# Making the shifted neighbour numbers on GpSimd instead of VectorE in a four-layer graph network

## The chip, the cores and the metric

The kernel runs on one core of one Trainium2 chip. The core has five engines that matter here: TensorE (PE, matrix products into PSUM), VectorE (DVE), ScalarE (ACT), GpSimd (POOL) and SyncE (SP, which issues nearly all DMAs). The metric is the device time of one execution in microseconds. Kernels are compared by the median of several runs.

## The reference, cut to what matters

128 graphs of 128 nodes with 64 features go through four layers, each `x = x + layer(max(layernorm(x), 0))`. Layer 0 is an edge network over the neighbours of each node; layers 1 to 3 multiply by the dense adjacency matrices and small weights.

```python
# layer 0, per graph; h is the normed input, mask = adj > 0
h_e = relu(xj_proj[:, None, :] + (h[:, None, :] - h[None, :, :]) @ W1b + b1)   # 192 wide
hm  = sum over neighbours k of h_e[j, k] * mask[j, k]
out = hm @ W2 + deg * b2
# layer 1: three graph convolutions relu(adj @ (h @ W + b)), then an output product
# layer 2: (adj @ h + h) @ W + b, rows scaled to length 1, batch norm over all graphs
# layer 3: tanh(concat(h, adj @ h) @ W1 + b1) @ W2 + b2
```

About an eighth of the entries of the adjacency matrices are nonzero, and the diagonal always is. Layer 0 is computed over the neighbours that are there, not over all pairs.

## The kernel before

**Tiling.** The graphs are worked in 32 groups of G = 4. A tile has the 128 nodes on the partitions, and the four graphs side by side. Layer 0 to layer 2 of all groups run in one software pipeline; layer 3 follows, because layer 2 has a batch norm over everything.

**Layer 0.** For every node the kernel numbers its neighbours. It sorts the rows by how many neighbours they have left beyond the first few, so that late neighbour slots are needed by few rows. The stage `sort` makes the tiles for this: `to` and `fro` (permutations into and out of the sorted order), `num` (for sorted row and column, the neighbour's number) and `num_r`. `num_r` is the tile of this case. Its 128 columns are cut into six segments of SEGS = 76, 33, 11, 4, 2 and 2 columns; every segment holds the first columns of `num` with a multiple of 3 taken off. One comparison with a constant then selects neighbour n in the first segment's rows, n + 3 in the second's, and so on. Four instructions make the first four segments (304, 132, 44 and 16 elements a partition, for four graphs); a fifth, with an operand `behind`, makes the last two together (16 elements).

The stage `pick` makes one-hot tiles by comparing `num`, `num_r` or `near_n` with a constant, all on VectorE. From group 1 on the twelve of a group come in this order: near 0, other 0, other 1, near 1, other 2, other 3, near 2, other 4, other 5, near 3, other 6, other 7. The near ones write `ohn` from `near_n` (`num` rearranged by way of DRAM); the others write `oh`, from `num` for other 0 to 4 and from `num_r` for other 5, 6 and 7.

Each group then has 40 half tiles (20 neighbour slots by two pairs of graphs), which go through five PSUM banks `blk`:

- `fill`: ScalarE copies `psort` (or `psort_r`, for the segments) into a bank;
- `subtract`: TensorE adds one-hot times `near_q` or `q` into the bank;
- `gather`: VectorE takes the relu and adds it to `acc` (half tiles 26 and 27 go by ScalarE).

Half tile h + 5 can be filled when half tile h is gathered. Below, "`acc` 23" is the VectorE instruction that gathers half tile 23. The stage `project` makes `q` and `psort` from the normed input (`x`, `sq`, `var`, `rstd`, `h`, `hT`); on GpSimd it makes the third part of `q`, `db` and `x+db`. The stage `after_layer0` ends layer 0 and does layers 1 and 2 (`sA`, `sB`, `ah`, `dT`, `msg`, `t`, `h`, `zT`, `sqy`, `nrm`, `counted`, `y`); its GpSimd work is `x+t`, `adjT+ident`, the mean's `x` and `y*nrm`.

**The order on the engines.** `keep_in_program_order` makes each engine run its instructions in the order in which they are emitted. That order comes from a timetable written out by hand. Each stage of each group is a generator; each piece up to the next `yield` has a due time (units of about 10 ns) from a plan, added to the group's start. Groups start PERIOD apart. `run_all` always emits the piece that is due first among those whose gate is open: a free PSUM bank, a tile made, a half tile gathered.

```python
    def due(self):
        k = min(self.k, len(self.plan) - 1)
        return self.start + self.scale * (self.plan[k] + 40 * (self.k - k))
...
        while streams:
            s = min((s for s in streams if s.gate is None or s.gate()), key=lambda s: s.due())
            s.step()
```

`sort` and `project` of a group run one period ahead of its half tiles, `after_layer0` one to two periods behind. The last entry of SORT_PLAN is the due time of `num_r`. First and last groups have other starts, scales and plans (MOVED, OWN); the change leaves these as they are.

Of the kernel before, what the change touches and what calls it, by code (L numbers as in the profile page):

```python
# [14 lines left out]
ALU = mybir.AluOpType  # L15
# [16 lines left out]
BLOCKS = 3  # L32
SEGS = [76, 33, 11, 4, 2, 2]
STARTS = [sum(SEGS[:s]) for s in range(len(SEGS))]
# [11 lines left out]
MOVED = {('pick', -1): (0, 0.75), ('pick', -2): (-109, 1.102), ('fill', -1): (18, 0.75), ('fill', -2): (0, 1.021), ('subtract', -1): (-1, 0.752), ('subtract', -2): (21, 0.988), ('gather', -1): (0, 0.75), ('gather', -2): (20, 1.0), ('pick', 0): (-1203, 0.997), ('fill', 0): (-119, 0.877), ('subtract', 0): (-65, 0.947), ('gather', 0): (-52, 0.511), ('sort', 0): (-364, 0.972), ('sort', 1): (-635, 0.697), ('project', 0): (691, 0.585), ('project', 1): (155, 0.997), ('after_layer0', 0): (0, 1.0), ('first_half', -1): (-602, 0.992), ('second_half', -1): (-112, 1.0)}  # L46
OWN = {('after_layer0', -2): [-734, -65, 691, 691, 691, 691, 691, 972, 1066, 1154, 1255, 1280, 1280, 1440, 1566, 1644, 1757, 1757, 1940, 1940, 2090, 2450, 2450, 2450, 2450, 2685, 2837, 2881, 3086, 3128, 3145, 3290, 3290, 3290, 3438, 3438, 3592, 3592, 3627, 3646, 3684, 3976, 4078, 4109, 4421, 4485, 4512, 4899], ('first_half', -1): [-1189, -966, -886, -871, -753, -659, -570, -311, -230, -110, -107, -26, -26, 24, 49, 159, 231, 233, 351, 355, 454, 465, 465, 520, 582, 606, 717, 717, 879, 909, 909, 998, 1084, 1149, 1238, 1238, 1283, 1313, 1390, 1404, 1404, 1660, 1664, 1695, 1824, 1984, 2001, 3035], ('second_half', -1): [-1130, -987, -834, -703, -655, -586, -484, -231, -231, -231, -109, -52, -17, 45, 104, 176, 245, 361, 361, 365, 470, 482, 482, 541, 607, 632, 750, 783, 934, 968, 968, 1168, 1168, 1222, 1321, 1321, 1368, 1391, 1493, 1493, 1493, 1734, 1786, 1832, 1980, 2117, 2144, 2459], ('sort', 0): [-361, 30, 30, 595, 607, 607, 738, 738, 860, 860, 860, 1135, 1135, 1235, 1331, 1331, 2024, 2074, 2074, 2134, 2159, 2159], ('project', 0): [-1241, -907, -868, -728, -442, 1053, 1192, 3091, 3728, 3875, 4077, 4162, 4162, 4162, 4182, 4512, 4589, 4619, 4619, 4651, 4662, 4902, 4978, 4996, 5074, 5127, 5127, 5664, 5780], ('pick', -1): [-1123, -774, -706, -706, -634, -425, -425, -96, -84, 631, 881, 881, 896, 1076, 1084, 1544, 1671, 1732, 2021, 2039, 2044, 2391, 2680, 2783, 2937, 3043]}
SET_UP_PLAN = [93, 1417, 1908, 1908, 2104, 2104, 3420, 4777]
PERIOD = 3386
SORT_PLAN = [-154, -48, 199, 202, 627, 627, 627, 929, 958, 958, 1091, 1091, 1251, 1452, 1457, 1527, 1567, 1663, 1680, 1736, 2145, 2323]  # L50
PROJECT_PLAN = [-3200, -3200, -3091, -3000, -2654, -2409, -881, 903, 903, 1198, 1371, 1474, 1614, 1698, 1832, 2224, 2239, 2239, 2335, 2335, 2471, 2516, 2579, 2723, 2943, 2976, 3375, 3417, 3511]
PICK_PLAN = [-1127, -907, -707, -689, -679, -577, -388, -388, -388, -31, 176, 734, 734, 1933]
FILL_PLAN = [-1179, -835, -192, -192, -192, -16, 194, 226, 527, 527, 666, 706, 715, 853, 1221, 1303, 1303, 1303, 1303, 1303, 1676, 1686, 1802, 1837, 1891, 1913, 1913, 1921, 1977, 2170, 2328, 2636, 2799, 2799, 2824, 2828, 2857, 2994, 2994, 3161, 3181]
SUBTRACT_PLAN = [-578, -369, -369, -369, -257, -40, -28, 354, 738, 738, 937, 937, 952, 952, 1114, 1123, 1130, 1476, 1567, 1688, 1688, 1746, 1860, 1936, 1978, 2041, 2068, 2293, 2349, 2448, 2623, 2758, 2868, 2868, 2926, 2939, 2939, 3072, 3078, 3201, 3238]
GATHER_PLAN = [-821, -801, -426, -156, -156, 267, 444, 479, 589, 589, 589, 1159, 1159, 1370, 1476, 1616, 1654, 1654, 1699, 1699, 1981, 1981, 2115, 2265, 2434, 2445, 2445, 2478, 2478, 2516, 2516, 2533, 2675, 2675, 2809, 2809, 2809, 2809, 2812, 2812, 2812]
AFTER_PLAN = [-115, -109, 110, 147, 311, 768, 891, 1024, 1031, 1342, 1462, 1486, 1666, 1825, 1907, 2009, 2138, 2138, 2250, 2401, 2571, 2571, 2663, 2805, 2902, 2973, 3117, 3221, 3537, 3748, 3892, 3907, 4155, 4155, 4155, 4239, 4331, 4381, 4557, 4586, 4665, 4760, 4834, 4915, 5251, 5412, 5494, 5494]
WARM = 15
BEHIND = 2
SPLIT = 1
# [49 lines left out]
def network(ctx, tc, io, out, over=None, x1=None):  # L109

    nc = Engines(tc)
# [218 lines left out]
    def set_up_first():  # L330

        yield
        nc.vector.tensor_scalar(wq, wp, -1.0, None, ALU.mult)
        nc.vector.tensor_tensor(wp, wp, wtop, ALU.add)
        done.add("w")
        yield
        centred(b2_all, F)
        yield from split_part(where["L0_gnn_b1"])
        for t in (near_q[1:] + near_n[1:]):
            nc.gpsimd.memset(t, 0.0)  # L340
        done.add("first")
        yield
# [191 lines left out]
    def sort(g):  # L534
# [70 lines left out]
        num = edge.tile([P, G, P], BF16, tag="num", name="num")  # L605
# [19 lines left out]
        yield  # L625
        num_r = edge.tile([P, G, P], BF16, tag="num_r", name="num_r")
        for i in range(LIKE):
            nc.vector.tensor_scalar(num_r[:, :, STARTS[i] : STARTS[i] + SEGS[i]], num[:, :, 0 : SEGS[i]], float(-i * BLOCKS), None, ALU.add)
        m, n = len(SEGS) - LIKE, SEGS[LIKE]
        nc.vector.tensor_tensor(  # L630
            num_r[:, :, STARTS[LIKE] : P].rearrange("p b (m n) -> p b m n", n=n),
            num[:, :, 0:n].unsqueeze(2).to_broadcast([P, G, m, n]),
            behind.unsqueeze(1).unsqueeze(3).to_broadcast([P, G, m, n]),
# [400 lines left out]
    if x1 is not None:  # L1034
        run(set_up_first())
        run(set_up())
        for g in range(NG - 1):
            run(after_layer0(g))
    else:
        streams = []  # L1040
        early = -9 * PERIOD
        streams.append(Stream(set_up_first(), SET_UP_PLAN, early))
        streams.append(Stream(set_up(), REST_PLAN, 0))
        for g in range(NG):
            for stage, plan, start in (
                (sort, SORT_PLAN, (g - 1) * PERIOD if g else early),
                (project, PROJECT_PLAN, (g - 1) * PERIOD if g else early),
                (pick, PICK_PLAN, g * PERIOD),
                (fill, FILL_PLAN, g * PERIOD),
                (subtract, SUBTRACT_PLAN, g * PERIOD),  # L1050
                (gather, GATHER_PLAN, g * PERIOD),
                *(((after_layer0, AFTER_PLAN, (g + 1) * PERIOD),) if g < NG - SPLIT else ((first_half, AFTER_PLAN, (g + 1) * PERIOD), (second_half, AFTER_PLAN, (g + 1) * PERIOD))),
            ):
                key = stage.__name__, g if g < 2 else g - NG
                later, scale = MOVED.get(key, (0, 1.0))
                streams.append(Stream(stage(g), OWN.get(key, plan), start + later, scale))
        streams.append(Stream(squares(), SQUARES_PLAN, (NG - 1) * PERIOD))
        streams.append(Stream(filler(), FILLER_PLAN, (NG - 1) * PERIOD))
        run_all(streams)
# [316 lines left out]
```

## Time and profile before

| what | value |
|---|---|
| median of 3 runs | 1288.45 us (1286.49 to 1288.77) |
| the profiled execution: its time | 1288.35 us |
| its span, first to last instruction | 1286.6 us |
| mean granted TensorE clock | 0.972 |
| instructions | 31407 |
| DVE `num_r`, the five forms together | 40.4 us busy in 160 instructions |

The profile is of one execution. Its time is 1.75 us longer than its span. A row such as `L93 DVE TENSOR_SCALAR num_r<-num 128x304 bf16<-128x304 bf16 x32 | 7.4, 230 | 0.0` reads: line, engine, operation, tile written <- tiles read, shapes, how many | busy us in all, mean ns of one | us that the engine stood idle just before them. The line is L93 for nearly all, since one helper emits everything, so the tiles tell the rows apart. `[0.47 <-PE blk L93]` in a timeline means that the engine stood idle 0.47 us until TensorE's `blk` was done.

### The profile page before, as it was taken

Reading aid. Unit: us, or ns where it says so; the run is one execution under the profiler, and the core shown is the slowest. Engines: PE = TensorE matmul, PEld = TensorE weight load, DVE = VectorE, ACT = ScalarE, POOL = GpSimd, SP = SyncE. Lnnn points to the kernel's source line nnn. Section 1 sums busy time; section 2 is a strip of 40 time slices with the busy share of each in tenths; the row PEclk is TensorE's granted clock in tenths of the full one; section 3 lists DMA queues with packets and bytes.
Section 4 is the critical chain, followed back from the end, with each engine's and each line's share of the span. In section 5 each row is a group of like instructions: output and inputs, shape, how many; then the busy total and the mean of one; then the engine's idle time right before and its main releaser. Section 6 shows DMA issues by size and latency. Waiting matters only on the chain.

```text
span 1286.6 us, 31407 instructions
## 1 busy us (share of the span) xinstructions
PE 1159.5 (90%) x10989; PEld 982.1 (76%) x10990; DVE 1158.9 (90%) x3204; ACT 1034.2 (80%) x2583; POOL 318.4 (25%) x400
## 2 busy tenths in 40 slices
PE   5689999999999999999999999999999999888697
PEld 2568888888877887787878878888878887767576
DVE  6889999999999999999999999999999998845993
ACT  3678888888988888888888888888988888743576
POOL 4241122212121222222211222221211222021992
PEclk9899999999999999999999999999999999995899
DMA  2222222222222222222222222222222212100264
GB/s 80 81 76 70 73 67 73 76 76 77 76 76 69 71 74 66 66 74 71 72 74 71 68 71 72 77 76 76 77 76 67 70 59 61 30 17 1 79 160 128
DMA packets 107012, 92.53 MB, mean 72 GB/s; under 512 B 45135, under 2 KB 90460, under 8 KB 106844
## 3 DMA queue, kind: packets, MB, share of 16 engines
q1 hardware_dynamic: 106380, 90.17, 24.7%
q8 instruction: 89, 1.46, 0.5%
q14 instruction: 79, 0.65, 0.2%
q10 hardware_dynamic: 464, 0.26, 0.1%
HBM read 34.12 MB, written 16.71 MB: 40 GB/s over the span
## 4 chain that ended last, share of the span: by engine, by line
ACT 40%; PE 35%; DVE 16%; issue 4%; POOL 2%; SPq 2%; DMA 1%; DVEq 0%; ACTq 0%; POOLq 0%
ACT blk L93 22%; PE blk L93 14%; PE ps_pr L93 7%; DVE acc L93 4%; ACT extra L93 3%; PE ps_q L93 3%; PE ps_ag L93 3%; ACT dT L93 3%; ACT msg L93 2%; PE ps_ah L93 2%; DVE var L93 2%; ACT psort L93 2%; PE ps_ga L93 2%; PE ps_endps L93 2%; SPq L93 2%
## 5 line engine op out<-in xcount | busy, mean ns | idle before, releaser
L93 DVE SCALAR_TENSOR_TENSOR acc<-blk,acc 128x384 f32<-128x384 f32 x1152 | 590.3, 548 | 28.3 <-PE blk L93 21.0
L93 ACT COPY blk<-psort 128x384 f32<-128x384 f32 x1088 | 497.6, 487 | 14.9 <-DVE acc L93 11.5
L93 PE MATMUL blk<-q,oh 128*128 128x192 bf16 x3072 | 321.9, 248 | 9.2 <-ACT blk L93 4.6
L93 PEld LDWEIGHTS <-oh 128*128 128x128 bf16 x3072 | 262.4, 99 | 43.7 <-issue 30.3
L93 PE MATMUL blk<-near_q,ohn 128*128 128x192 bf16 x1536 | 227.7, 247 | 35.9 <-ACT blk L93 32.3
L93 PEld LDWEIGHTS <-ohn 128*128 128x128 bf16 x1536 | 142.8, 99 | 94.9 <-issue 83.3
L93 POOL TENSOR_TENSOR x<-x,t 128x260 f32<-128x260 f32 (+1 forms) x33 | 23.9, 726 | 426.8 <-DVE t L93 372.7
L93 ACT COPY blk<-psort_r 128x384 f32<-128x384 f32 x192 | 89.1, 490 | 1.9 <-DVE acc L93 0.8
L93 ACT COPY zT<-ps_ga 128x256 f32<-128x256 f32 (+1 forms) x31 | 11.4, 369 | 87.5 <-PE ps_ga L93 87.5
L93 POOL TENSOR_TENSOR y<-y,nrm 128x256 f32<-128x256 f32 x31 | 20.4, 657 | 245.4 <-PE blk L93 214.9
L93 PE MATMUL ps_ag<-adjT,msg 128*128 128x128 f32 x500 | 73.7, 280 | 0.5 <-ACT msg L93 0.5
L93 PE MATMUL ps_pr<-g,dT 128*128 128x128 f32 x496 | 72.9, 279 | 0.3 <-ACT dT L93 0.2
L93 DVE TENSOR_SCALAR ohn<-near_n 128x1536 bf16<-128x1536 bf16 (+1 forms) x132 | 72.0, 546 | 0.0
L93 PEld LDWEIGHTS ps_pr<-g,dT 128*128 128x128 f32 x496 | 65.0, 191 | 4.4 <-ACT dT L93 1.6
L93 PEld LDWEIGHTS ps_ag<-adjT,msg 128*128 128x128 f32 x500 | 63.3, 192 | 0.9 <-ACT msg L93 0.7
L93 ACT ACTIVATE dT<-ps_ag 128x512 f32<-128x512 f32 (+1 forms) x96 | 56.5, 588 | 8.6 <-PE ps_ag L93 8.6
L93 DVE SCALAR_TENSOR_TENSOR h<-x,rstd 128x256 f32<-128x256 f32 (+1 forms) x98 | 51.9, 530 | 9.8 <-PE ps_ga L93 2.0
L93 ACT ACTIVATE sq<-x 128x256 f32<-128x256 f32 (+1 forms) x98 | 40.4, 412 | 25.1 <-DVE x L93 25.0
L93 POOL TENSOR_TENSOR q<-rest,q 128x768 bf16<-128x768 f32 x32 | 52.7, 1648 | 18.2 <-ACT q L93 18.2
L93 PE MATMUL ps_q<-wq,hT 128*128 128x384 f32 x128 | 55.5, 518 | 1.4 <-ACT hT L93 1.4
L93 PE MATMUL ps_p<-wp,hs 128*128 128x384 f32 x128 | 53.8, 503 | 0.1
L93 PE MATMUL ps_sA<-fro,acc 128*128 128x128 f32 x256 | 50.7, 280 | 1.3 <-DVE acc L93 1.3
(267 smaller groups left out, 2605.0 us busy)
## 6 DMA issues: line engine op xcount, KB each, us to landing
near_q<-q SPq DMA_DIRECT2D x288, 63.0 KB
near_n<-n_dram SPq DMA_DIRECT2D x96, 126.0 KB
a<-in_adj_dram SPq DMA_DIRECT2D x32, 256.0 KB
adjT_dram<-adjT SPq DMA_DIRECT2D x32, 256.0 KB
adjT<-adjT_dram SPq DMA_DIRECT2D x32, 256.0 KB
psort_r<-psort SPq DMA_DIRECT2D x32, 228.0 KB
fro_r<-fro SPq DMA_DIRECT2D x32, 152.0 KB
x<-in_x_dram SPq DMA_DIRECT2D x32, 128.0 KB
```

The costliest lines, as they stand in the source:

```text
L93: ins = op(*args, **kw)
```

## The change

The five instructions that make `num_r` are issued to GpSimd and not to VectorE. The plans of the steady period are replaced by others and PERIOD goes from 3386 to 3384; thereby the order on every engine changes in places. The reads of `num_r` stay on VectorE.

```diff
-PERIOD = 3386
-SORT_PLAN = [-154, -48, 199, 202, 627, 627, 627, 929, 958, 958, 1091, 1091, 1251, 1452, 1457, 1527, 1567, 1663, 1680, 1736, 2145, 2323]
-PROJECT_PLAN = [-3200, -3200, -3091, -3000, -2654, -2409, -881, 903, 903, 1198, 1371, 1474, 1614, 1698, 1832, 2224, 2239, 2239, 2335, 2335, 2471, 2516, 2579, 2723, 2943, 2976, 3375, 3417, 3511]
-PICK_PLAN = [-1127, -907, -707, -689, -679, -577, -388, -388, -388, -31, 176, 734, 734, 1933]
-FILL_PLAN = [-1179, -835, -192, -192, -192, -16, 194, 226, 527, 527, 666, 706, 715, 853, 1221, 1303, 1303, 1303, 1303, 1303, 1676, 1686, 1802, 1837, 1891, 1913, 1913, 1921, 1977, 2170, 2328, 2636, 2799, 2799, 2824, 2828, 2857, 2994, 2994, 3161, 3181]
-SUBTRACT_PLAN = [-578, -369, -369, -369, -257, -40, -28, 354, 738, 738, 937, 937, 952, 952, 1114, 1123, 1130, 1476, 1567, 1688, 1688, 1746, 1860, 1936, 1978, 2041, 2068, 2293, 2349, 2448, 2623, 2758, 2868, 2868, 2926, 2939, 2939, 3072, 3078, 3201, 3238]
-GATHER_PLAN = [-821, -801, -426, -156, -156, 267, 444, 479, 589, 589, 589, 1159, 1159, 1370, 1476, 1616, 1654, 1654, 1699, 1699, 1981, 1981, 2115, 2265, 2434, 2445, 2445, 2478, 2478, 2516, 2516, 2533, 2675, 2675, 2809, 2809, 2809, 2809, 2812, 2812, 2812]
-AFTER_PLAN = [-115, -109, 110, 147, 311, 768, 891, 1024, 1031, 1342, 1462, 1486, 1666, 1825, 1907, 2009, 2138, 2138, 2250, 2401, 2571, 2571, 2663, 2805, 2902, 2973, 3117, 3221, 3537, 3748, 3892, 3907, 4155, 4155, 4155, 4239, 4331, 4381, 4557, 4586, 4665, 4760, 4834, 4915, 5251, 5412, 5494, 5494]
+PERIOD = 3384
+SORT_PLAN = [-133, -27, 220, 296, 645, 645, 645, 936, 965, 965, 1098, 1098, 1258, 1452, 1452, 1527, 1663, 1663, 1663, 1736, 2145, 2457]
+PROJECT_PLAN = [-3200, -3200, -3098, -3007, -2661, -2347, -819, 965, 965, 1191, 1364, 1467, 1607, 1691, 1879, 2217, 2232, 2232, 2278, 2278, 2414, 2459, 2666, 2666, 2886, 2984, 3375, 3417, 3511]
+PICK_PLAN = [-1178, -1121, -947, -668, -658, -556, -436, -436, -436, -79, 106, 323, 530, 1969]
+FILL_PLAN = [-1185, -933, -54, -54, -54, -54, 174, 203, 504, 504, 601, 618, 703, 1079, 1320, 1320, 1320, 1320, 1320, 1379, 1572, 1716, 1850, 1850, 1904, 1926, 1928, 1961, 1991, 1991, 2087, 2650, 2838, 2864, 2864, 2887, 2887, 3036, 3036, 3044, 3252]
+SUBTRACT_PLAN = [-570, -570, -570, -570, -464, -390, -390, 362, 746, 746, 943, 943, 943, 943, 943, 1114, 1444, 1444, 1534, 1688, 1688, 1746, 1874, 1874, 1874, 2031, 2061, 2380, 2380, 2479, 2652, 2787, 2894, 2894, 2921, 2924, 2938, 2938, 2947, 2947, 2958]
+GATHER_PLAN = [-819, -819, -553, -332, -332, 215, 446, 447, 447, 678, 698, 1268, 1268, 1401, 1507, 1605, 1639, 1685, 1730, 1860, 2033, 2033, 2167, 2312, 2481, 2518, 2518, 2551, 2551, 2589, 2618, 2618, 2789, 2789, 2789, 2789, 2810, 2884, 2884, 2884, 2884]
+AFTER_PLAN = [-112, -106, 113, 150, 234, 771, 894, 1039, 1066, 1379, 1465, 1489, 1666, 1847, 1929, 2031, 2160, 2160, 2272, 2401, 2538, 2538, 2663, 2805, 2902, 2973, 3103, 3211, 3527, 3733, 3897, 3899, 4064, 4145, 4156, 4204, 4321, 4399, 4598, 4627, 4797, 4892, 4966, 5034, 5383, 5544, 5544, 5544]
...
         for i in range(LIKE):
-            nc.vector.tensor_scalar(num_r[:, :, STARTS[i] : STARTS[i] + SEGS[i]], num[:, :, 0 : SEGS[i]], float(-i * BLOCKS), None, ALU.add)
+            nc.gpsimd.tensor_scalar(num_r[:, :, STARTS[i] : STARTS[i] + SEGS[i]], num[:, :, 0 : SEGS[i]], float(-i * BLOCKS), None, ALU.add)
         m, n = len(SEGS) - LIKE, SEGS[LIKE]
-        nc.vector.tensor_tensor(
+        nc.gpsimd.tensor_tensor(
             num_r[:, :, STARTS[LIKE] : P].rearrange("p b (m n) -> p b m n", n=n),
...
```

## The prediction

> **What bounds the kernel now.** I read the page first, then one period of the steady part.
>
> ```profile
> PE 1159.5 (90%) x10989; PEld 982.1 (76%) x10990; DVE 1158.9 (90%) x3204; ACT 1034.2 (80%) x2583; POOL 318.4 (25%) x400
> ```
>
> Two engines are at 90% of the span, so the average does not say which of them holds the clock. The groups by tile put the `num_r` instructions of the steady groups exactly one period apart (605.09, 639.17, 673.25 us): 34.08 us. From group 2 (93.30 us) to group 31 (1081.87 us) there are 29 periods. I cut the one from 639.17 us in two, at the first `acc` of the next group (651.71 us), with the busy time by windows (engine, busy us, number):
>
> ```profile
> core 0: us, PE busy (x) PEld busy (x) DVE busy (x) ACT busy (x) POOL busy (x), PEclk, DMA share, GB/s
> 639.17:651.71 12.54, 12.54 (x120) 11.31 (x120) 11.60 (x31) 12.40 (x31) 3.65 (x4) 1.00 0.35 97
> 651.71:673.25 21.54, 19.51 (x194) 16.14 (x192) 21.19 (x57) 17.23 (x45) 3.20 (x4) 1.00 0.20 58
> ```
>
> This carries the prediction. In the first 12.54 us TensorE has no idle time and ScalarE 0.14 us, while VectorE has 0.94 us. In the other 21.54 us VectorE is short of full by 0.35 us only, and TensorE waits 2.03 us. The period is a ring: VectorE sets the pace from `acc` 0 to about `acc` 21 (671.78 us), then ScalarE and TensorE until TensorE hands over the next `acc` 0. `num_r` stands just behind the point where the ring leaves VectorE. The waits from 468.5 to 809.6 us (ten periods) agree:
>
> ```profile
> PE blk L93 <- ACT blk L93: 10.6, 28, 0.9
> PE ps_ga L93 <- DVE h L93: 7.4, 10, 0.7
> DVE acc L93 <- PE blk L93: 8.0, 21, 0.5
> ACT zT L93 <- PE ps_ga L93: 29.8, 10, 3.0
> ```
>
> TensorE and ScalarE wait for VectorE's `h` (the layer-2 norm); VectorE waits 0.8 us a period for TensorE's `blk`, and that is where `num_r` is.
>
> **What is taken away.** Five VectorE instructions per group. VectorE's timeline, a usual period and one at 264 us:
>
> ```profile
> 639.17 0.49 DVE L93 TENSOR_SCALAR num_r<-num 128x304 bf16<-128x304 bf16 x4
> 639.57 0.59 DVE L93 TENSOR_TENSOR num_r<-num,behind 128x16 bf16<-128x16 bf16 x1
> 643.55 0.56 DVE L93 SCALAR_TENSOR_TENSOR acc<-blk,acc 128x384 f32<-128x384 f32 x1 [0.47 <-PE blk L93]
> 264.44 0.17 DVE L93 TENSOR_TENSOR num_r<-num,behind 128x16 bf16<-128x16 bf16 x1
> 267.34 0.56 DVE L93 SCALAR_TENSOR_TENSOR acc<-blk,acc 128x384 f32<-128x384 f32 x1 [0.35 <-PE blk L93]
> ```
>
> The queue gets from the first of them (639.17) to the next `acc` (640.09) in 0.92 us: 0.40 for four starts, 0.52 for the last. Times 29 that is 26.7 us, 2.1%, which would be the gain if VectorE were the bound there. It is not, and the trace has the trial already: at 264 us the last instruction took 0.17 us and not 0.59, `acc` 23 began at 264.53, 0.49 us after the first and not 0.92, and 2.8 us later VectorE waited 0.35 us for `blk`. `num_r` stands at 264.04 and 298.12 us, so that period was again 34.08 us. 0.43 us less VectorE time bought nothing. I take 0 for the removal; its upper bound, were all of it on the ring, is -26.7 us.
>
> **What is added on GpSimd.** Four TENSOR_SCALAR and one TENSOR_TENSOR per group. Due times put them behind `y*nrm` (2160) and `q` (2232), ahead of `db` (2459) and `x+db` (2666). The nearest rows, from the groups by shape:
>
> ```profile
> L93 POOL TENSOR_SCALAR c<-c,ident 3x449 bf16<-3x449 bf16 x2 | 2.8, 1411 | 0.2
> L93 POOL TENSOR_SCALAR c<-c,ident 3x128 bf16<-3x128 bf16 x2 | 1.5, 750 | 0.2
> L93 POOL TENSOR_SCALAR in_n<-neg_p 128x1 f32<-128x1 f32 x6 | 1.3, 220 | 2.2 <-DVE upto_t L93 1.9
> L93 POOL TENSOR_TENSOR x<-x,t 128x260 f32<-128x260 f32 x31 | 23.0, 740 | 424.6 <-DVE t L93 370.5 <-DMA psort_r<-psort 54.1
> ```
>
> From the first two: (1411-750)/321 = 2.06 ns an element and 486 ns fixed, so 304, 132, 44 and 16 elements cost 1.11, 0.76, 0.58 and 0.52 us. `x+t` (740 ns at 260 elements, 494 at 130) leaves about 0.28 us for the last. Sum 3.2 us. Low end: 220 ns fixed and the 0.76 ns an element of the cast `to` (609 ns for 512) give 1.26 + 0.2 = 1.5 us. I take 3.2, since the `c` rows are the same operation on the same type. GpSimd is busy 6.85 of 34.08 us, so it stays at 30%. Cover: `q` ends at 641.75, `num_r` is then done by 645.0, and its first reader, other 5, starts at 653.58: 8.6 us. Behind it `db` and `x+db` move from 643.2 to about 646.4; the next GpSimd instruction starts at 656.74, and `x+db` is read a period later. No DMA is moved: the third spread of `q` is issued ahead of `num_r`, and the load for `near_q`'s first use has landed at 683.32 for a use at 685.35.
>
> **The port.** The timeline has `num_r`'s last instruction ending with GpSimd's `y*nrm` (640.16 and 640.14), and VectorE's `h` beside `db` taking 0.86 us where 0.42 is usual (641.75); an `ohn` that began beside the end of `q` and `db` (1050.46) took 0.68 and not 0.55. So GpSimd's instructions hold up some of VectorE's. Their run grows from 639.48-643.21 to about 639.5-646.4. In it lie `h` (already held 0.44), other 0 and other 1 (644.49, 644.69) and near 1 (645.36); near 0 comes forward from 644.02 into `num_r`'s place. Bounds for one: 0 and the GpSimd instruction met (1.11, or 1.65 for `q`). Taken: 0.2 for near 0, 0.3 more for `h`, 0.25 each for the others: 1.25 us. Cover on the same stretch: the freed 0.92 and the wait of 0.47: 1.39 us. So I cost it at nothing; without that cover it would be up to 1.25 x 29 = 36 us.
>
> The Trainium skill speaks against the change here: "SBUF — State Buffer", section "Who interferes with whom", says that VectorE and GpSimd share a port pair, that a copy, cast or tensor_scalar in its fast two-port form, or an instruction with two SBUF inputs, is locked out for the whole GpSimd instruction. The held `h` and `num_r` are two-input ones and agree, at 0.44 and 0.43 us; by that rule the one-hots would be held as well, and the sum above already has them.
>
> **The redrawn order.** Sorting the due times, with the gates, gives each queue's order for both tables. On VectorE the set from `acc` 0 to `acc` 21 stays, but `spare_n` (0.07) now comes ahead of `acc` 21, the layer-2 square root on ScalarE goes behind the copy `ah`, and `nrm` max waits for it. `ah` ends at 671.53 and the root takes 0.22, against 671.29 now: a wait of 0 to 0.45; `ah` may come earlier because `acc` 16 goes behind `h1`, so 0.15. In return `acc` 14 passes the `rest` that waits 0.14 us for ScalarE, and `zT` goes behind four fills, which closes TensorE's small waits for `blk` (0.17, 0.36, 0.53 between 663.5 and 668.4). TensorE gains from that only what VectorE follows: at most its gaps there, 0.17 us. Sum: 0.07 + 0.15 - 0.17 = +0.05 us a period, 29 x 0.05 = +1.5 us. Head and tail keep their own tables; taken as 0, bound 1 us either way, as an odd period (570.74 to 605.09) was 0.28 us long.
>
> The profiled execution took 1288.35 us (span 1286.6 and 1.75 around it), 0.10 under the median of 1288.45. 1288.35 + 1.5 = 1289.8 us.
>
> **The rivals.**
>
> *Shorter ring.* The table closes the waits of 663-668 us and VectorE, 0.92 us lighter, keeps up. About half of the 1.06 us: -0.5 x 29 = -14.5, about 1274 us. For it: TensorE idles 2.03 us a period, all in that stretch. Against: VectorE has 0.35 us of slack in it, and nothing leaves it.
>
> *The port, slower.* Near 0 now stands where `y*nrm` and `q` run. It also reads `near_n`, whose last DMA's semaphore is full at 673.59, 0.34 after `num_r`'s place (673.25). If it waits so long that `q` (1.65) starts ahead of it, it loses about 1.5, and with `h`, other 0, other 1 and near 1 (1.05) the sum is 2.5 against a cover of 1.39; half of the rest is made up at later waits: +0.55 x 29 = +16, about 1304 us. It decides when the holds pass 1.39 us a period.
>
> *Not what it says.* If the first reader waited for `num_r`, GpSimd would need 8.6 us more; no row comes near that. Chance nil.
>
> **How the numbers follow.** Forecast 0.46: -0.15 to +0.25 us a period, 1284 to 1296. Shorter 0.24, port 0.30. 0.2% is 2.6 us, about what a measurement of this kernel can tell from no change. Of the forecast's 0.46, 0.24 lies within it, 0.07 below, 0.15 above; with the rivals: faster 0.31, same 0.24, slower 0.45. Range 1274 (the middle of the shorter case) to 1306 (just past the port case): 0.12 and 0.08 are left out.
>
> **What would show it.** Right: `num_r` on POOL at about 3 us a group behind `q`; VectorE busy 1120 to 1145 us and a longer wait of `acc` for `blk`; a period of 34.0 to 34.3 us; other 5 never waiting. Port: `ohn`, `oh` and `h` means well above 549, 285 and 557 ns, and `blk` waiting for `acc`. Shorter: less of PE `blk` <- ACT `blk` and a period under 33.9. Wrong altogether: a VectorE wait on POOL `num_r`, or a period changed with those rows unchanged.

## The result and the profile after

| | before | after |
|---|---|---|
| median of 6 runs each | 1287.32 us (1286.25 to 1288.77) | 1294.97 us (1293.41 to 1296.04) |
| the profiled execution: time, span | 1288.35, 1286.6 us | 1294.71, 1292.9 us |
| steady period | 34.075 us | 33.875 us |

The ratio is 1.0055, with a 95% interval of 1.0045 to 1.0066: slower by 0.6%, though the period became shorter. The first part of the page, for the kernel after:

```profile
PE 1167.7 (90%) x10990; PEld 977.4 (76%) x10990; DVE 1146.5 (89%) x3044; ACT 1036.8 (80%) x2583; POOL 405.4 (31%) x560
```

VectorE has 160 instructions less and GpSimd 160 more, so the change does what it says. VectorE lost 12.4 us of busy time although the forms of `num_r` sum to 40.4. In the trace they overlap one another and their neighbours: without them VectorE would be busy 1135.2 us and not 1158.9, so 23.7 us were theirs alone. Of that the near one-hots took back 17.7 (72.0 us before; their mean in the steady periods before was 549 ns), while `h` took 7.7 less (51.9 before, 44.3 after). The near one-hots and `num_r` in the list of the page after:

```profile
L93 DVE TENSOR_SCALAR ohn<-near_n 128x1536 bf16<-128x1536 bf16 (+1 forms) x132 | 89.7, 681 | 6.1 <-DMA near_n<-n_dram 5.3
L93 POOL TENSOR_SCALAR num_r<-num 128x304 bf16<-128x304 bf16 (+3 forms) x128 | 76.6, 605 | 5.8 <-ACT num L93 1.8
```

The waits of ten steady periods (466.9 to 805.7 us), the rows that answer to those of before. Of the four rows shown for before, three are gone (TensorE for ScalarE's `blk`, TensorE for VectorE's `h`, ScalarE for TensorE's `ps_ga`); now VectorE waits in other places and ScalarE waits for VectorE:

```profile
DVE acc L93 <- PE blk L93: 4.3, 9, 0.5
DVE spare_n L93 <- PE blk L93: 3.7, 7, 0.5
DVE ohn L93 <- DMA near_n<-n_dram: 1.2, 3, 0.6
PE ps_o L93 <- DVE degs L93: 6.5, 10, 0.7
ACT blk L93 <- DVE acc L93: 29.3, 30, 2.3
```

One period of the kernel after, in VectorE's timeline and then in GpSimd's. Near 0 (642.66) and near 1 (647.89) take longer than 0.55 (near 0 stands beside GpSimd's `y*nrm`, 642.40 to 643.02); the two `oh` at 646.93 take their usual 0.49 together although GpSimd works on `num_r` all that time; and the first reader of `num_r`, other 5 at 656.46, comes 8.7 us after `num_r` is done and waits for nothing:

```profile
642.66 0.78 DVE L93 TENSOR_SCALAR ohn<-near_n 128x1536 bf16<-128x1536 bf16 x1
645.13 0.61 DVE L93 SCALAR_TENSOR_TENSOR h<-x,rstd 128x256 f32<-128x256 f32 x1
646.93 0.49 DVE L93 TENSOR_SCALAR oh<-num 128x512 bf16<-128x512 bf16 x2
647.89 0.85 DVE L93 TENSOR_SCALAR ohn<-near_n 128x1536 bf16<-128x1536 bf16 x1
656.46 0.28 DVE L93 TENSOR_SCALAR oh<-num_r 128x512 bf16<-128x512 bf16 x1
```

```profile
643.41 1.65 POOL L93 TENSOR_TENSOR q<-rest,q 128x768 bf16<-128x768 f32 x1 [0.39 <-ACT q L93]
645.03 2.44 POOL L93 TENSOR_SCALAR num_r<-num 128x304 bf16<-128x304 bf16 x4
647.53 0.22 POOL L93 TENSOR_TENSOR num_r<-num,behind 128x16 bf16<-128x16 bf16 x1
647.71 0.63 POOL L93 TENSOR_TENSOR db<-degs,b_all 128x260 f32<-128x260 bf16 x1
```

**Where the time went.** The ScalarE cast that writes `num` comes once a group, so its 32 starts in the trace (numbered from 0) are a clock for the whole program. The same was done for every kernel of the experiments; their rows are read later. Differences to the kernel before, us (its own times in the first row):

| kernel | num 2 | num 29 | num 31 | last `acc` | end |
|---|---|---|---|---|---|
| before | 87.95 | 1008.11 | 1075.27 | 1128.32 | 1286.56 |
| after | +6.31 | +1.20 | +3.09 | +5.30 | +6.36 |
| e1_move_only | +1.00 | +15.10 | +15.59 | +16.72 | +14.75 |
| e2_plans_only | +7.17 | +2.05 | +3.74 | +5.73 | +4.14 |
| e3_left_out | +1.83 | +2.95 | +2.97 | +2.70 | +0.28 |
| e11_sa_only | +2.14 | -1.50 | +0.39 | +1.17 | -0.89 |
| e12_combined | +2.76 | -2.74 | -2.57 | -0.44 | -0.36 |

So the kernel after loses 6.31 us in its first 94 us, wins 5.11 back in 27 periods (0.19 each), and loses 4.10 from num 29 to the last `acc` and 1.06 in layer 3. The last column also holds the noise of layer 3: from the last `acc` to the end, kernels that have the same plan there differ by up to 3.5 us in this table. Each row is one execution. The granted TensorE clock is 1.00 between num 2 and num 29 in all of them, so the periods can be compared as they stand; up to num 2 it is between 0.78 (e2) and 0.90 (before), so a difference of 1 or 2 us in the head need not come from the order. e3, with the old plans, has +1.83 there.

### The profile page after: what moved, and what is told of

It reads as the page before. It is cut to its first block, busy times and chain, and to the rows that moved or that the text cites. A ratio compares the mean times of both kernels' runs of the same rounds, so it can differ in the third digit from the quotient of the medians.

```text
span 1292.9 us, 31475 instructions
## 1 busy us (share of the span) xinstructions
PE 1167.7 (90%) x10990; PEld 977.4 (76%) x10990; DVE 1146.5 (89%) x3044; ACT 1036.8 (80%) x2583; POOL 405.4 (31%) x560
## 3 DMA queue, kind: packets, MB, share of 16 engines
HBM read 34.12 MB, written 16.71 MB: 39 GB/s over the span
## 4 chain that ended last, share of the span: by engine, by line
PE 57%; DVE 25%; ACT 9%; issue 3%; POOL 3%; SPq 2%; DMA 1%; DVEq 0%; ACTq 0%; POOLq 0%
PE blk L93 26%; PE ps_pr L93 9%; DVE acc L93 8%; PE ps_ag L93 7%; ACT blk L93 5%; PE ps_sA L93 4%; PE ps_p L93 4%; DVE h L93 2%; DVE var L93 2%; PE ps_q L93 2%; SPq L93 2%; PE ps_endps L93 2%; DVE lower L93 1%; DVE rank L93 1%; DVE rank_t L93 1%
## 5 line engine op out<-in xcount | busy, mean ns | idle before, releaser
L93 PE MATMUL blk<-q,oh 128*128 128x192 bf16 x3072 | 325.9, 248 | 13.0 <-ACT blk L93 4.8
L93 PE MATMUL blk<-near_q,ohn 128*128 128x192 bf16 x1536 | 223.8, 247 | 13.9 <-ACT blk L93 12.5
L93 PEld LDWEIGHTS <-ohn 128*128 128x128 bf16 x1536 | 139.0, 98 | 78.4 <-issue 63.5
L93 DVE TENSOR_SCALAR ohn<-near_n 128x1536 bf16<-128x1536 bf16 (+1 forms) x132 | 89.7, 681 | 6.1 <-DMA near_n<-n_dram 5.3
L93 POOL TENSOR_SCALAR num_r<-num 128x304 bf16<-128x304 bf16 (+3 forms) x128 | 76.6, 605 | 5.8 <-ACT num L93 1.8
L93 PE MATMUL ps_ag<-adjT,msg 128*128 128x128 f32 x508 | 70.0, 280 | 0.5 <-ACT msg L93 0.5
L93 POOL TENSOR_TENSOR q<-rest,q 128x768 bf16<-128x768 f32 x32 | 53.6, 1674 | 26.5 <-ACT q L93 17.7
L93 POOL TENSOR_TENSOR x<-x 128x256 f32<-128x256 f32 (+1 forms) x33 | 19.8, 601 | 111.3 <-DVE h L93 103.6
L93 POOL TENSOR_TENSOR y<-y,affine_g 128x256 f32<-128x256 f32 x62 | 44.2, 733 | 28.4 <-DVE affine_g L93 26.7
```

Source lines behind the costliest of these rows:

```text
L93: ins = op(*args, **kw)
```

## The experiments

There were three questions: what the move to GpSimd does by itself, what the redrawn plans do by themselves, and what loses the time in the head and the tail. The theories, with the letters that some expectations use: the redrawn plans alone make the difference, in the ends (E: the first and last groups are to blame as a whole; H1: one copy, `sA` of group 0, stands wrongly in ScalarE's queue); against it, A': the redrawn order needs the relief of VectorE; P: the place of `num_r` in GpSimd's queue makes the price of the move.

**e1_move_only: old plans, `num_r` on GpSimd.**

```diff
# before.py
-            nc.vector.tensor_scalar(num_r[...
+            nc.gpsimd.tensor_scalar(num_r[...
-        nc.vector.tensor_tensor(
+        nc.gpsimd.tensor_tensor(
```

> The old plans, with the five num_r instructions on GpSimd. Theory A (the removal lies outside the ring; the redrawn order shortened the period): the period stays 34.08 us, VectorE waits about 0.9 us longer for blk, time within 2 us of before (1286 to 1290). Theory B (the 0.92 us of VectorE that came free shortened the period by 0.20 us): period about 33.88 us, time about 1281 to 1283. Theory C (the port): one-hots or h held longer than is covered, period over 34.2 us, over 1291.

Measured: 1303.82 us, ratio 1.0116 [1.0101, 1.0131]; the period is 34.56 us. Alone, the move costs 0.48 us a period. VectorE's timeline in a usual period, then a row of TensorE's and three of GpSimd's:

```profile
651.07 0.43 DVE L93 SCALAR_TENSOR_TENSOR h<-x,rstd 128x256 f32<-128x256 f32 x1 [0.90 <-PE ps_ga L93]
651.90 0.56 DVE L93 SCALAR_TENSOR_TENSOR acc<-blk,acc 128x384 f32<-128x384 f32 x1 [0.40 <-PE blk L93]
652.98 0.56 DVE L93 SCALAR_TENSOR_TENSOR acc<-blk,acc 128x384 f32<-128x384 f32 x1 [0.53 <-PE blk L93]
653.46 0.55 DVE L93 TENSOR_SCALAR ohn<-near_n 128x1536 bf16<-128x1536 bf16 x1
653.92 0.93 DVE L93 TENSOR_SCALAR oh<-num 128x512 bf16<-128x512 bf16 x2
655.25 0.70 DVE L93 TENSOR_SCALAR ohn<-near_n 128x1536 bf16<-128x1536 bf16 x1
```

```profile
650.37 0.66 PE L93 MATMUL ps_ga<-to,h 128*64 128x128 f32 x8
649.53 1.65 POOL L93 TENSOR_TENSOR q<-rest,q 128x768 bf16<-128x768 f32 x1
653.60 0.48 POOL L93 TENSOR_TENSOR num_r<-num,behind 128x16 bf16<-128x16 bf16 x1
654.04 0.67 POOL L93 TENSOR_TENSOR db<-degs,b_all 128x260 f32<-128x260 bf16 x1
```

Without `num_r` ahead of it, `h` could start 0.9 us earlier, but it waits for TensorE, as the profile says: the tile of `h` has one buffer, and TensorE's `ps_ga` still reads the `h` of the group before. It ends at 651.03, and `h` starts 0.05 us later. The same 0.90 us opens in e3 and e5, and in twelve periods of each of the three kernels `h` starts 0.05 us after `ps_ga` has ended. TensorE holds the ring at that place, so the freed time is gone before anything used it: 0.90 us ahead of `h`, then 0.40 and 0.53 ahead of two `acc`, where the kernel before waits 0.47 ahead of one. Behind them come the holds: the two `oh`, other 0 and other 1, take 0.93 us and not 0.49, as other 1 meets `db`, and near 1 takes 0.70 and not 0.55. The starts of the `acc` within one period, counted from `acc` 0, show where the 0.48 arises (medians of 18 periods; the numbers count VectorE's own `acc` instructions from 0, so that from 26 on the half tile's number is two higher):

```
acc            20     23     27     28     29     31     next 0
before      19.12  22.45  25.91  27.26  28.19  29.18   34.08
e1_move_only  +.01   -.90   +.01   +.47   +.62   +.57    +.48
e3_left_out   +.01   -.90   +.01   +.01   +.02   +.01    +.01
e5_move_later +.01   -.90   +.01   +.34   +.37   +.31    +.23
after         -.22   +.19   -.18   -.56   -.10   -.16    -.20
e2_plans_only -.21   +.69   +.07   -.41   -.41   -.15    -.17
```

In e1 the gain of 0.90 at `acc` 23 is nothing at `acc` 27. A loss of 0.46 appears at `acc` 28, which stands right behind other 0 and other 1, and of 0.15 more at `acc` 29, right behind near 1. That is what these one-hots were held, and most of it stays. e3, without any `num_r`, has the same gain, loses it at the same place, and has no loss behind it: the price of the move is the holds.

**e2_plans_only: new plans, `num_r` still on VectorE.** 
```diff
# after.py
-            nc.gpsimd.tensor_scalar(num_r[...
+            nc.vector.tensor_scalar(num_r[...
-        nc.gpsimd.tensor_tensor(
+        nc.vector.tensor_tensor(
```

> The new plans, with num_r left on VectorE. Theory A in its plain form (the order alone made the shorter period): period about 33.88 us and the ends' loss, 1294 to 1297. Theory A' (in the new order ScalarE waits 2.9 us a period for acc, so VectorE is the ring at num_r's place and needs the relief): period 34.4 to 34.8, i.e. 0.5 to 0.9 us more than after, 1308 to 1322. Theory B expects 34.08 and about 1301.

Measured: 1294.48 us, ratio 1.0051 [1.0035, 1.0067], period 33.88 to 33.91 us. That is the result of the whole change. In the new order the engine of `num_r` is worth nothing that can be measured, and A' falls: the redrawn order does not need the relief. The +6 us of the head and the tail's loss are here as well (table above).

**e3_left_out and e6_left_out_new: `num_r` not made at all**, with the old and the new plans; the last one-hots compare `num` instead of `num_r`, which leaves out the shift of the numbers.

```diff
-        num_r = edge.tile([P, G, P], BF16, tag="num_r", name="num_r")
-        ...
-        sorts[g] = num, num_r, fro, fro_r
+        sorts[g] = num, num, fro, fro_r
```

> The old plans; num_r is not made at all, and other 5 to 7 compare num itself (the shift of the neighbour numbers is left out). The upper bound of what the removal can give under the old order. Theory A: period 34.08, time 1286 to 1289. Theory B: period 33.2 to 33.9, 1260 to 1282.

> The changed kernel's plans with no num_r made at all (other 5 to 7 compare num itself; the shift is left out). If num_r is off the ring of the new order on either engine: period 33.85 to 33.90, as in after (33.88) and e2 (33.88 to 33.91), 1293 to 1296. If the holds of near 0 and near 1 in after are on the ring and cancel a gain: about 33.4 to 33.6, 1281 to 1287.

Measured: e3 1289.05 us, ratio 1.0005 [0.9994, 1.0016], period 34.085 us: taking all of `num_r` away buys nothing in the old order. Its `acc` 23 comes 0.90 us earlier and its `acc` 27 at the old time, as in e1. e6: 1295.44 us, 1.0051 [1.0038, 1.0064], period 33.88 us, the same as e2, but for two odd periods of 35.45 and 35.49 us in its profile, with a near 0 held to 1.85 and 1.95 us. So `num_r` lies off the ring in both orders.

**e5_move_later: e1 with `num_r` behind `db` and `x+db` on GpSimd.**

```diff
# before.py with num_r on GpSimd
-SORT_PLAN = [..., 2145, 2323]
+SORT_PLAN = [..., 2145, 2590]
```

> The old plans with num_r on GpSimd, as in e1, but its due time 2323 is 2590, so that it stands behind x+db in GpSimd's queue; no other engine's order changes. Theory P (in e1 GpSimd's num_r, db and x+db hold other 1 and near 1 just behind the acc that waits for blk, and acc 30 has no slack, which costs 0.48 us a period): behind x+db it meets accs, which do not share the port, and one-hots later on, where VectorE waits for blk anyway; period 34.1 to 34.3, 1287 to 1294. Theory Q (any num_r on GpSimd costs, wherever it stands, by semaphores or by db and x+db coming late): 34.5 and 1302 to 1305.

Measured: 1295.83 us, 1.0065 [1.0049, 1.0081], period 34.30 us. The time is 2 us above what P expected, the period at its upper end. Half of e1's 0.48 us is gone, with the same instructions on the same engines, so theory P holds for that half. The other half is the same kind of loss in another place: the one-hots now stand beside `num_r` itself and are held by it. VectorE and GpSimd:

```profile
647.66 0.69 DVE L93 TENSOR_SCALAR ohn<-near_n 128x1536 bf16<-128x1536 bf16 x1
648.27 0.67 DVE L93 TENSOR_SCALAR oh<-num 128x512 bf16<-128x512 bf16 x2
646.97 2.52 POOL L93 TENSOR_SCALAR num_r<-num 128x304 bf16<-128x304 bf16 x4
```

In nine periods near 0 takes 689 ns, other 0 371 and other 1 378, which is 0.32 us more than unheld, and `acc` 28 right behind them comes 0.34 us late.

**e4_head_later: the whole stage `after_layer0` of group 0 later by 60 units.**

```diff
-('after_layer0', 0): (0, 1.0)
+('after_layer0', 0): (60, 1.0)
```

> The changed kernel with one number more: after_layer0 of group 0 starts 60 units later (MOVED), so that its copy sA comes behind the extra of group 1 in ScalarE's queue, as before the change. Theory H1 (the head lost 6.3 us by num 2 because ScalarE stood 2.7 us at sA, whose buffer the set-up on GpSimd holds until 76.5 us, with extra and the fills queued behind it): num 2 comes 2.5 to 5 us earlier than 94.3 us, the time is 1290 to 1292.5; the steady period stays 33.88. Theory H2 (the head lost because GpSimd's set-up ends 0.9 us later behind num_r): num 2 moves by less than 1 us, 1294 to 1296.

Measured: 1297.9 us, 1.0066 [1.0054, 1.0079]. Num 2 comes 2.3 us earlier than in the kernel after, but from num 2 to num 3 it takes 38.91 us where the kernel after takes 33.55. A stage of 48 pieces was moved for the sake of one of them, and the others broke the next period: e11 below, which moves that one alone, takes 33.54 us there.

**e7_hybrid_ends and e8_hybrid_vec: the old plans for the first two and last two groups**, the new ones between; `num_r` on GpSimd (e7) or VectorE (e8).

```diff
                 later, scale = MOVED.get(key, (0, 1.0))
+                plan = OLD[stage.__name__] if g < 2 or g >= NG - 2 else plan
```

> The changed kernel, with the old plans for all stages of the first two and the last two groups. Theory E (the redrawn plans lose their gain at the ends, whose own tables were made for the old plans): num 2 within 2 us of before's 87.9, the steady period 33.88, the end as before: 1281 to 1286, faster than both. Rival S (seams between the two tables cost as much as they bring): 1288 to 1295.

> As e7, with num_r on VectorE. Theory E: the same period (33.88 to 33.91), 1281 to 1286, within 2 us of e7; where the old plans stand, num_r on VectorE saves up to 0.5 us a period against e7. If the engine matters in the new order: more than 3 us from e7.

Measured: e7 1294.37 us, 1.0044 [1.0028, 1.0059]; e8 1294.23 us, 1.0041 [1.0028, 1.0054]. E falls as a remedy: e8's num 2 is at +0.34, so the old plans do mend the head, but two odd periods of 35.44 us and the seam at the tail cost as much (last `acc` +6.28, end +10.3; the profile is of e8's slowest execution, 1298.63 us). One of those odd periods, in VectorE's timeline of e8 (L101 is this kernel's line for the same helper):

```profile
436.29 1.56 DVE L101 TENSOR_SCALAR ohn<-near_n 128x1536 bf16<-128x1536 bf16 x1 [0.50 <-DMA near_n<-n_dram]
```

Near 0 waited for the DMA of `near_n`, GpSimd's `q` began meanwhile, and near 0 then took 1.56 and not 0.55 us. That is the mechanism of the rival "The port, slower"; it comes now and then, not in each period.

**e9_near0_back and e10_near0_vec: near 0 back at its old due time**, in the new plans, with `num_r` on GpSimd (e9) or VectorE (e10).

```diff
-PICK_PLAN = [-1178, -1121, -947, ...
+PICK_PLAN = [-1178, -1121, -707, ...
```

> The changed kernel with one due time put back: near 0 is due at -707 again and not at -947, so that it stands behind acc 30, where it stood before. Theory N (near 0 came forward to the edge of near_n's landing; where it misses, GpSimd's q starts first and near 0 is held: 1.5 us in odd periods and always in the period of group 30): no near 0 over 1 us or waiting for near_n, period 30 to 31 is 33.1 to 33.9 and not 35.0, 2 to 4 us faster than after if the steady period stays 33.88. Rival (near 0 now stands among GpSimd's num_r, as other 1 and near 1 did in e1, so the steady period becomes 34.0 to 34.5): 1294 to 1304.

> As e9, with num_r on VectorE. Theory N without GpSimd's num_r in the way: no held near 0, period 33.85 to 33.95, period 30 to 31 33.1 to 33.9, 1289 to 1292 (the head's loss of 6 to 7 us stays). Rival: with 0.9 us of num_r and near 0 in the old place VectorE is the ring and the period goes back to 34.1, 1296.

Measured: e9 1293.58 us, 1.0050 [1.0036, 1.0063], period 33.96; e10 1294.71 us, 1.0050 [1.0037, 1.0063], period 33.87. No near 0 of the middle is held any more. But the head still loses (num 2 +6.95 and +8.15), and near 0 of group 30 is still held, 2.01 and 1.63 us, so that num 30 to 31 takes 34.58 and 34.55 us where 33.1 to 33.9 was expected. The time did not move. e9 shows one thing more, VectorE and then GpSimd:

```profile
646.35 1.02 DVE L93 SCALAR_TENSOR_TENSOR h<-x,rstd 128x256 f32<-128x256 f32 x1
648.96 0.55 DVE L93 TENSOR_SCALAR ohn<-near_n 128x1536 bf16<-128x1536 bf16 x1
649.43 0.49 DVE L93 TENSOR_SCALAR oh<-num 128x512 bf16<-128x512 bf16 x2
650.30 0.74 DVE L93 TENSOR_SCALAR ohn<-near_n 128x1536 bf16<-128x1536 bf16 x1
```

```profile
647.06 2.70 POOL L93 TENSOR_SCALAR num_r<-num 128x304 bf16<-128x304 bf16 x4
650.00 0.63 POOL L93 TENSOR_TENSOR db<-degs,b_all 128x260 f32<-128x260 bf16 x1
```

`h` starts while `q` is still under way, 0.74 us before its end, and takes 1.02 us where 0.43 is usual: a held VectorE instruction stands in the profile as a longer one. Near 0 and two `oh` run inside `num_r` at their usual times. The four `num_r` take 2.70 us here and 2.44 in the kernel after, where no near 0 stands beside them. Near 1, beside `db`, is held by 0.19.

**e11_sa_only: the kernel after with one due time changed**, for group 0 alone.

```diff
-OWN = {
+OWN = {('after_layer0', 0): [-112, -106, 113, 150, 290, 771, ...],   # AFTER_PLAN with 234 -> 290
```

> The changed kernel with one due time of one group: the copy sA of group 0 alone is due 56 units later, behind the four extra of group 1 on ScalarE; e4 had moved the whole stage. Theory H1: num 2 comes 2 to 4 us earlier than after's 94.3 us, and the next period stays about 33.5, so 1291 to 1293. Rival H3 (the head's loss has several causes, and what waits behind sA waits next for something else): num 3 moves by less than 1 us, 1294 to 1296.

Measured: 1288.01 us (12 runs), ratio 1.0009 [0.9996, 1.0022]. One number in one group gives back most of the 0.55%. Entry 4 of AFTER_PLAN is ScalarE's copy `sA`. In the kernel before it was due at 3386 + 311 = 3697, behind `extra` 2 and 3 of group 1 (3655); in the kernel after at 3384 + 234 = 3618, ahead of them. ScalarE's queue before, after, and in e11 at that place:

```profile
72.36 0.81 ACT L93 ACTIVATE extra<-psort,spare_n 128x192 f32<-128x192 f32 x2
73.08 2.95 ACT L93 COPY blk<-psort 128x384 f32<-128x384 f32 x7
75.96 0.58 ACT L93 COPY sA<-ps_sA 128x512 f32<-128x512 f32 x1
```

```profile
76.53 0.59 ACT L93 COPY sA<-ps_sA 128x512 f32<-128x512 f32 x1 [2.73 <-POOL own_graph L93]
77.01 0.80 ACT L93 ACTIVATE extra<-psort,spare_n 128x192 f32<-128x192 f32 x2
77.72 2.94 ACT L93 COPY blk<-psort 128x384 f32<-128x384 f32 x7
```

```profile
73.77 0.80 ACT L93 ACTIVATE extra<-psort,spare_n 128x192 f32<-128x192 f32 x2
74.47 2.94 ACT L93 COPY blk<-psort 128x384 f32<-128x384 f32 x7
77.36 0.57 ACT L93 COPY sA<-ps_sA 128x512 f32<-128x512 f32 x1
```

The buffer of `sA` (the tag `sA`) is lent to `c3`, a tile of the set-up's work on GpSimd, which ends near 76 us in all these kernels (75.6 before, 76.5 after). Before, the seven fills went ahead and the copy came just when the buffer was free. After, the copy stands ahead of them and ScalarE waits 2.73 us with `extra` and seven fills behind it. VectorE then waits for the first `acc` of group 1, in its timeline before and after:

```profile
74.04 1.02 DVE L93 SCALAR_TENSOR_TENSOR acc<-blk,extra 128x384 f32<-128x384 f32 x2 [1.10 <-ACT blk L93]
```

```profile
78.83 1.02 DVE L93 SCALAR_TENSOR_TENSOR acc<-blk,extra 128x384 f32<-128x384 f32 x2 [5.84 <-PE blk L93]
```

The time is better than the 1291 to 1293 us that H1 expected. In e11 num 2 comes 4.2 us earlier than in the kernel after, which is most of the head's 6.31; 2.1 stay, where e3 has 1.83 with the old plans, and an odd period of 35.67 us in the middle takes 1.8 of the gain. By the ratios the two kernels differ by 0.46%, or 5.9 us, with both intervals about 0.1% wide to either side; the 4.2 of the head are shown, the rest isn't placed. The clock does not explain them: up to num 2 it is 0.87 in the kernel after and 0.89 in e11, and e12, which has the same due time, is 3.5 us ahead of the kernel after at num 2 with 0.81. H1 holds for the larger part.

**e12_combined: each loss that was placed, undone**: new plans, `num_r` on VectorE, near 0 back, `sA` as in e11, and group 30's near 0 behind GpSimd's `q`.

```diff
+OWN = {('pick', -2): [-1178, -1121, -543, ...],   # near 0 of group 30, -947 -> -543
```

> The new plans with num_r on VectorE, near 0 at its old due time (-707), the copy sA of group 0 behind extra 2,3 of group 1 (due 290), and near 0 of group 30 behind the third part of q (due -543 in a plan of its own). Each edit is aimed at one loss that an earlier run placed. If these losses add (theory: single places in the order, one by one): num 2 some 2 us later than in the kernel before, 27 periods of 33.87 give 27 x 0.21 = 5.7 back, so num 29 about 3.5 us earlier than before; group 30's near 0 at 0.55 us and no wait of 1 us, so period 30 to 31 near 33.5 and not 35; the end 3 to 4 us earlier: 1283 to 1286 us, ratio 0.996 to 0.998. Rival (every seam asks its price again, as in the runs with a head or ends of their own): the head comes out right but another wait opens behind the moved near 0 or in the odd periods: 1287 to 1292 us, no faster than before.

Measured: 1287.15 us (12 runs), against 1287.77 us of the kernel before (17 runs): ratio 0.9993 [0.9984, 1.0003]. Period 33.87 us with one of 34.12; group 30's near 0 takes 0.55 and num 30 to 31 33.45 us where the kernel after has 35.04 and e10, which differs from e12 only in `sA` and in this near 0, 34.55. At num 29 the kernel is 2.74 us ahead and at num 31 2.57. From there to the last `acc` it needs 55.19 us where the kernel before needs 53.05, and all but 0.44 of the lead is given back. The expectation of 1283 to 1286 missed by that tail, which no run took apart. No kernel of the study is shown to be faster than the one before.

## Why the prediction was right or wrong, point by point

The direction was right and the time lies within the range, but 5 us above the forecast, and by other terms than the sum had. That the direction came out right is luck: in the steady part, which the sum was about, the period became shorter, and the time was lost in the ends, which the sum put at nothing.

**The ring, and a removal worth nothing: right.** e3 shows it best: without `num_r` the period is 34.085 us. The trial read from one short instruction at 264 us told the truth. The row behind it, which the prediction did not read, also tells where the freed time goes, to the wait for TensorE ahead of `h` that e1, e3 and e5 have in each period:

```profile
266.51 0.47 DVE L93 SCALAR_TENSOR_TENSOR h<-x,rstd 128x256 f32<-128x256 f32 x1 [0.42 <-PE ps_ga L93]
```

**GpSimd's price: within its bounds, a little high.** Forecast 3.2 us a group out of 1.5 to 3.2; the rows by shape for ten periods of the kernel after:

```profile
L93 POOL TENSOR_SCALAR num_r<-num 128x304 bf16<-128x304 bf16 x10 | 11.6, 1161 | 0.0
L93 POOL TENSOR_SCALAR num_r<-num 128x132 bf16<-128x132 bf16 x10 | 5.4, 544 | 0.0
L93 POOL TENSOR_SCALAR num_r<-num 128x44 bf16<-128x44 bf16 x10 | 4.2, 417 | 0.6
L93 POOL TENSOR_SCALAR num_r<-num 128x16 bf16<-128x16 bf16 x10 | 2.9, 293 | 0.6
L93 POOL TENSOR_TENSOR num_r<-num,behind 128x16 bf16<-128x16 bf16 x10 | 2.2, 219 | 0.6
```

They sum to 2.63 us a group. The 1.11 us taken from the `c` rows for the first was close (1.16); the fixed part of 486 ns was too high (293 ns for 16 elements).

**The port: right that it costs nothing in the new order, wrong in its parts and in its cover.** Forecast holds: near 0 0.2, `h` 0.3 more, other 0, other 1 and near 1 0.25 each, in all 1.25 us. Measured as means of the same one in nine steady periods: near 0 733 ns (+0.18), near 1 975 (+0.43), other 0 and 1 nothing, and the held `h` 486 ns where it had 818 before (-0.33), in all 0.28. The Trainium skill, "SBUF — State Buffer", section "Who interferes with whom", says that whoever starts first takes the shared pair for its whole instruction (the prediction gave only the half in which VectorE loses); by that, what counts is the instruction that is under way and how long it is. The runs agree in both directions. One-hots that come upon a running GpSimd instruction are held: 1.56 to 2.01 us for a near 0 caught by `q` in e8 and e9, 0.70 for near 1 beside `x+db` in e1, 0.69 for near 0 beside the longest `num_r` in e5. GpSimd instructions that come upon a running one-hot are held themselves: in e2 `q` starts 0.03 us after near 0 and takes 2.03 us where 1.65 is usual, while near 0 takes its 0.55, and `num_r`'s last form took 480 ns beside near 0 in e1 and 219 in the kernel after. There the `oh` came ahead of a short form of `num_r` and ran nearly free, 291 ns for 58 of them against 282 alone. That the give and take goes by who started first is argued from these starts and durations; no run forced the order. The cover of 1.39 us was wrong for the old order: the 0.92 us went into the wait for `ps_ga`, the waits for `blk` stand ahead of the one-hots, and nothing covered the holds of 0.42 and 0.15 behind them, so e1 lost 0.48 us a period. In the kernel after `acc` 28 comes 0.56 us earlier, and near 1's hold of 0.43 leaves `acc` 29 still 0.10 ahead.

**The redrawn order: wrong sign, small.** Forecast +0.05 us a period, measured -0.20. The term that failed is the claim that TensorE's gaps bound the gain (0.17) while VectorE's part loses 0.22 (0.07 and 0.15). The table of `acc` starts has it: from `acc` 0 to `acc` 20 VectorE is 0.22 us shorter with the same 48 instructions, 0.14 of it the wait of `rest` for ScalarE, which the prediction had named and not counted; the other 0.08 isn't placed. e2 shows that the plans alone do it; that it is this wait is read from the timelines, and no run changed that place alone. `spare_n` and `nrm` went as foreseen in order, but they stand behind `acc` 20, where the ring has left VectorE, so their +0.22 was no cost. From `acc` 20 to the next `acc` 0 the kernels take 14.96 and 14.98 us.

**The head and the tail "taken as 0, bound 1 us": this step failed.** It said that head and tail keep their own tables. Only the stages in OWN do; those in MOVED take the new plans with another start and scale, and `after_layer0` of group 0 takes them with neither. So the first and last groups were redrawn too, against a set-up that was not. The bound came from an odd period in the steady part, which says nothing of the ends. Measured: +6.31 us by num 2, of which e11 traces 4.2 to the copy `sA`, and +4.10 from num 29 to the last `acc`. Of the latter 1.95 is in the step from num 30 to num 31, where group 30's near 0 stands (MOVED draws it forward by 109 and 1.102): in VectorE's timeline of the kernel after

```profile
1050.79 1.70 DVE L93 TENSOR_SCALAR ohn<-near_n 128x1536 bf16<-128x1536 bf16 x1 [1.03 <-DMA near_n<-n_dram]
```

and in e12, with that near 0 moved, the step is 1.59 us shorter, 1.10 of it against e10. A hold there is not a loss in itself: e1 and e3, with the old plans, have a near 0 of 1.59 us in this step, and it takes 33.09 us as before. The other 2.2 us, after num 31, is open; it is in e12 too. In e11, whose VectorE has the same order there as the kernel after, it is only 0.78 us: the kernel after ran its last 4.2 us up to the last `acc` at a granted clock of 0.79, and e11 its last 3.0 at 1.00. But the kernel before has such a stretch as well (0.73 from 1124 to 1129 us), so how much of the 2.2 us is the order's is not shown.

The terms, 1288.35 + 6.31 - 5.11 + 4.10 + 1.06 = 1294.71, add up to the time of the profiled execution because they are pieces of the two traces; that proves no cause. The last 1.06, in layer 3, is within what kernels with the same layer 3 differ by.

**The rivals.** "Shorter ring" was partly true, -0.20 and not -0.5 us a period: its two signs, a period under 33.9 us and less of TensorE's waits for ScalarE's `blk`, are both there, and the ends cost more than it won. "The port, slower" has the right mechanism (near 0 misses the landing, `q` begins first, 1.5 us) but it does not recur in each period: the kernel after has it in group 30, and e4, e6, e7, e8 and e11 have it in one or two odd periods, e6 without any `num_r`. e11's at 741 us:

```profile
741.31 1.70 DVE L93 TENSOR_SCALAR ohn<-near_n 128x1536 bf16<-128x1536 bf16 x1 [1.03 <-DMA near_n<-n_dram]
```

## What to carry to other kernels

Before costing a moved step, find which engine carries the ring at its place: the starts of one recurring instruction, counted from the first of its period, showed in one table what a gain of 0.90 us was worth four `acc` later. When a plan for the steady part is redrawn, follow every stage that inherits it into the first and last periods, and look in each in-order queue for a copy whose buffer something else still holds: one due time in one group cost 4 us, where the move itself cost nothing in the new order. An offload wants its own place in the order: the same five instructions on GpSimd cost 0.48 us a period, half of that, or nothing, by where they and their neighbours stood. And read the releaser that the profile names for an idle time before looking for another one: a coincidence in time, here of the start of `h` in e1 with the end of `q`, is not a cause, and the program's buffers (one for `h`) told the two apart.

## What the runs showed of the hardware that was not expected

Whether a VectorE one-hot was held beside a GpSimd instruction went with which of the two was under way first. Beside `num_r` the one-hots ran at their usual times in e9 (550 ns for near 0, 283 and 282 for the `oh`), where they came ahead of a short form or met its end, and were held in e5 (689, 371 and 378 ns), where they came upon its two longer forms. Beside `q`, `db` and `x+db` they were held (742 ns on average for near 1 in e9, 975 in the kernel after, 549 unheld). The hold also runs the other way: in e9 the form of `num_r` with 16 elements took 606 ns beside near 0 and an `oh`, where 254 was its time in e1.

A hold stood in the profile as a longer instruction: `h`, started while `q` ran, took 1.02 us in e9 where 0.43 is usual. The idle time of 0.90 us ahead of `h` in e1 was something else, a wait for TensorE to have read the only buffer.
